# Layer norm at the end of a four-layer kernel: the variance by squares of the projection, gamma by GpSimd, and the residual added two pairs later

## The chip, the cores and the metric

One core of a Trainium2 chip runs one program over 16 images. The metric is the device time of one execution, in microseconds (us). The engines are PE (TensorE: matmuls, with weight loads as PEld), DVE (VectorE), ACT (ScalarE), POOL (GpSimd) and SP (SyncE, which here only issues DMAs). Each engine takes its instructions strictly in its own order; between engines there are semaphores.

## The reference

The input is `x`, 16 images of 64 x 64 pixels with 256 channels, float32. Four layers run one after the other, each as `x = x + layer(groupnorm(x))`. What the change touches is the last, linear attention with a layer norm:

```python
q, k, v = split(einsum('bxyc,cf->bxyf', x, w_qkv), 3)      # 128 channels each: 4 heads of 32
q = softmax(q, over the 32 channels of a head) * DIM_HEAD ** -0.5
k = softmax(k, over the 4096 pixels)
context = einsum('bhdn,bhen->bhde', k, v)
out = einsum('bhde,bhdn->bhen', context, q)
out = einsum('bxyh,hc->bxyc', out, w_out) + b_out
mu = mean(out, over the 256 channels); var = mean(square(out - mu))
out = (out - mu) * rsqrt(var + 1e-3) * gamma + beta
```

The layers before it: a search for the nearest of 1024 codes for each pixel, whose code is added (layer 0); an attention with sigmoids inside each row of 64 pixels (layer 1); and a gate from a softmax over 4096 x 4096 products of two rows, with which the pixel is multiplied (layer 2).

## The kernel before

Each image passes through generators, one for each stage: `stats0` (group norm statistics), `stage1` (search), `layer1`, `rows2`, `stage2` (the exponentials of layer 2), `gate2` and `stage3` (layer 3). A loop at the end of the kernel interleaves them. Every stage of every image has a start and a length written out by hand, every `yield` a weight, and the loop always continues the generator with the earliest due time. So five images are in work at once: while `stage3` finishes image 7, `gate2` works on image 8, `stage2` on image 9, `layer1` on image 10 and `stage1` on image 11. The scheduler of the language then settles the order in each engine's queue, near to the order of emission; work under `tc.high_priority` is pulled ahead. PE's order therefore has matmuls of four stages between two of `stage3`.

Tiles come from pools in which the tiles of one tag share a few buffers. In PSUM all stages share four banks of 128 x 512 float32 (`bank`) and two double banks (`wide`, for the search's distances and for layer 1).

A pixel set of 512 is a chunk; an image has eight. Images are kept in DRAM between the stages, channels on partitions (`x3` for `stage3`). `stage3` has two halves.

The first half goes over the chunks for keys, queries and values. With channels on partitions as weights, one matmul pair for each 128 pixels gives q and v side by side (L759). The group norm's mean comes in as a row that is added by a matmul with three rows of ones in bfloat16 (`ones3`, L763): `qv_row`, 256 wide, for two tiles at a time. ACT copies the bank to `qv` (L764, tag `u4`), POOL subtracts the maximum of each head (L779), ACT takes the exponential (L780), POOL multiplies by the reciprocal sum (L728), PE transposes q, and the result `qT` goes to DRAM (`qd`). The product of keys and values is summed up in `ctxa` (L784, L786).

Between the halves a short chain of URGENT steps (L797 to L817) transposes the context, masks it to the heads, multiplies it by `w_out`, scales it by the sum of the keys (`rk`, L805) and adds the bias `bo`. `w_out` and the bias were centred over the channels at the start, so the projection has mean zero, and its variance is the mean of its squares. Two forms of the weight are kept: `wctx[:, 0]` without gamma and `wctx[:, 1]` with it. From the first, two transposes and two matmuls make the Gram matrix `gram` = W W^T / 256.

The second half, the output half, goes over the chunks again. `form` (L822 to L828) loads the chunk's q, multiplies it by `gram` (`pz`, L826) and lets DVE multiply the product by q (`qz`, L828). `variance` (L830 to L837) sums this over the channels by a matmul with a column of ones (`pvr`, L834); ACT adds epsilon (L836) and POOL raises to -0.5 (L837): `rss`, the reciprocal deviation of each pixel. Both work one chunk ahead. Then, for each pair of 128-pixel tiles: PE projects with the weight that has gamma (`po`, L854), ACT scales each tile by its deviation on the way out of PSUM (L857, to `y`, tag `u4`), PE transposes the chunk of `x3` (`xo`) into a bank and adds the row `x_row` with beta (`pxo`, L859 and L863), and DVE adds both (L865). SP stores the chunk before (L867).

Outside layer 3 the change touches the search, `stage1`: for each tile of 128 pixels, ACT writes `nn` (L372), PE the distances `pd` (L377), DVE adds the two into `nd` and takes the maximum (L384), DVE finds its index (L389), and POOL issues the gather that adds the code row to the tile of pixels (L390). The pixels of a chunk are transposed back by PE (L352, `pt`) once its last gather has landed. `sq`, `nn`, `nd`, `fg` and `rows` share the tag `t4`; `qT`, `kx`, `ek` and `qz` share `v2`. In `stage2`, ACT and DVE take turns on 128 x 2048 exponentials: L617 on ACT, L620 on DVE with two inputs in SBUF.

Of the kernel before, what the change touches and what calls it, by code (L numbers as in the profile page):

```python
# [9 lines left out]
F32 = mybir.dt.float32  # L10
BF16 = mybir.dt.bfloat16
U32 = mybir.dt.uint32
AF = mybir.ActivationFunctionType
ALU = mybir.AluOpType
AX = mybir.AxisListType

P = 128
# [24 lines left out]
def kernel(  # L42
# [55 lines left out]
    neg_mat = s1p.tile([P, P], F32, tag="t4", name="neg_mat", bufs=5)  # L98
# [26 lines left out]
    def row_tile(name):  # L125
        t = const.tile([P, C], BF16, name=name)
        nc.gpsimd.memset(t, 0.0)
        return t

    h_row, qv_row, x_row = row_tile("h_row"), row_tile("qv_row"), row_tile("x_row")  # L130

    def twice(row):
        return row.unsqueeze(1).to_broadcast([P, 2, C])

    def put_row(dst, v, weight, tag, plus=None):
# [4 lines left out]
        row = pb[:PARTS, :C]  # L140
        weight(row, v3, plus)

        for n in range(PARTS - 1):
            top = small.tile([PARTS, C], BF16, tag="ptop", name=f"top_{tag}_{n}", bufs=1)
            nc.scalar.copy(top, row)
            nc.tensor.matmul(row, lhsT=below[:, n, :], rhs=top, start=False, stop=True, skip_group_check=True)
# [70 lines left out]
    for n in range(PARTS):  # L217
        nc.scalar.dma_start(out=bh3[:, :, n], in_=bh.rearrange("(k p) -> p k", p=P))
    one = const.tile([P, 1], F32, name="one")
# [83 lines left out]
    def stage1(b):  # L303
# [14 lines left out]
        def norm(ch):  # L318
            xn[ch] = s1p.tile([P, NK, CW], F32, tag="xn", name=f"xn_{tag}_{ch}")
            sq = s1p.tile([P, NK, CW], F32, tag="t4", name=f"sq_{tag}_{ch}", bufs=5)  # L320
# [46 lines left out]
        for ch in range(NCHUNK):  # L367
            for t in range(CH):
                T = ch * CH + t

                nn = s1p.tile([P, CODES], F32, tag="t4", name=f"nn_{tag}_{T}", bufs=5)
                nc.scalar.activation(nn, ne2, AF.Identity, bias=nx2[ch][:, t : t + 1])  # L372
                pd = wide(f"pd_{tag}_{T}")
                for hf in range(2):
# [7 lines left out]
                nd = s1p.tile([P, CODES], F32, tag="t4", name=f"nd_{tag}_{T}", bufs=5)  # L382
                m8 = m8s[T % 4]
                nc.vector.tensor_tensor_reduce(  # L384
                    out=nd, in0=pd, in1=nn, scale=1.0, scalar=-3.0e38, op0=ALU.add, op1=ALU.max,
# [3 lines left out]
                nc.vector.max_index(i8, m8, nd)  # L389
# [26 lines left out]
    def layer1(b):  # L416
# [34 lines left out]
        def attend(ch):  # L451
# [9 lines left out]
            fg = s1p.tile([2 * CK, 2, HW], F32, tag="t4", name=f"fg_{tag}_{ch}", bufs=5)  # L461
# [78 lines left out]
    def rows2(b):  # L540
# [17 lines left out]
        for h in range(2):  # L558
# [9 lines left out]
            rows = s1p.tile([P, CW], F32, tag="t4", name=f"rows_{tag}_{h}", bufs=5)  # L568
# [120 lines left out]
    def stage3(b):  # L689
# [9 lines left out]
        with tc.high_priority(offset=URGENT):  # L699
            scaled(wk_n, scale, nc.scalar)  # L700
            scaled(wqv_n, scale, nc.vector)
            put_row(qv_row, nmean, by_weight(wqv_n), f"qv_{tag}")
# [9 lines left out]
        def queries(ch):  # L712
# [4 lines left out]
            qT = s3p.tile([P, CW], F32, tag="v2", name=f"qT_{tag}_{ch}", bufs=4)  # L717
# [12 lines left out]
        for ch in range(NCHUNK):  # L730
# [14 lines left out]
            kx = s3p.tile([P, CW], F32, tag="v2", name=f"kx_{tag}_{ch}", bufs=4)  # L745
# [6 lines left out]
            qv = s3p.tile([P, CH, 2, P], F32, tag="u4", name=f"qv_{tag}_{ch}")  # L752
            qvs[ch] = qv
            for pr in range(CH // 2):
# [8 lines left out]
                nc.tensor.matmul(pqv, lhsT=ones3, rhs=twice(qv_row), start=False, stop=True, skip_group_check=True)  # L763
# [7 lines left out]
            ek = s3p.tile([P, CH, P], F32, tag="v2", name=f"ek_{tag}_{ch}", bufs=4)  # L771
# [23 lines left out]
        with tc.high_priority(offset=URGENT):  # L795
            pt = bank(f"pct_{tag}")
            nc.tensor.transpose(pt[:, :P], ctxa, ident)  # L797
            ctx_bd = wts.tile([P, P], F32, tag="ctx_bd", name=f"ctxbd_{tag}")
            nc.vector.tensor_tensor(ctx_bd, pt[:, :P], hmask, ALU.mult)
# [3 lines left out]

            wctx = wts.tile([P, 2, C], F32, tag="wctx", name=f"wctx_{tag}")
            nc.vector.scalar_tensor_tensor(wctx[:, 0, :], pw[:, :C], rk, bo, op0=ALU.mult, op1=ALU.add)  # L805
            nc.vector.tensor_tensor(wctx[:, 1, :], wctx[:, 0, :], gam, ALU.mult)

            pw = bank(f"pwt_{tag}")
            for k in range(NK):
                nc.tensor.transpose(pw[:, k * P : (k + 1) * P], wctx[:, 0, k * P : (k + 1) * P], ident)  # L810
            wT = wts.tile([P, NK, P], F32, tag="wk_n", name=f"wT_{tag}")
            nc.scalar.copy(wT.rearrange("p k d -> p (k d)"), pw[:, : NK * P])
            pw = bank(f"pgr_{tag}")
# [131 lines left out]
```

## Time and profile before

| what | us | where from |
|---|---|---|
| time, median of three runs | 5938.17 | runs from 5902.65 to 5948.46 |
| profiled execution | 5928.44 | its own time |
| its span | 5926.7 | first to last instruction |
| granted TensorE clock, mean | 0.941 | of full speed |
| first residual addition (L865) of images 7 and 8 | 3621.5 and 3972.8 | L865's row of starts |
| POOL's product with the query sums (L728), median and longest | 1.049 and 3.201 | L728's row |
| DVE's product with the exponentials (L620), median | 2.282 | L620's row |

How such a profile is read: for every engine it has the busy time and its share of the span, for every group of instructions (line, engine, operation, tiles) the count, the busy time, the mean duration and the idle time of the engine just before, with what ended it. A float32 matmul of this kernel shows as two passes, each with a weight load. A list of waits says which engine stood still for which other; a "window" is the same count for a stretch of the span. Busy shares are means over stages with different limits, so the stretches below are taken from one image's cycle.

In the middle of the span the cycle repeats for each image; the first image (before its followers start) and the last four (5005 us on) run with fewer partners.

### The profile page before, as it was taken

Reading aid. Unit: us, or ns where it says so; the run is one execution under the profiler, and the core shown is the slowest. Engines: PE = TensorE matmul, PEld = TensorE weight load, DVE = VectorE, ACT = ScalarE, POOL = GpSimd, SP = SyncE. Lnnn points to the kernel's source line nnn. Section 1 sums busy time; section 2 is a strip of 40 time slices with the busy share of each in tenths; the row PEclk is TensorE's granted clock in tenths of the full one; section 3 lists DMA queues with packets and bytes.
Section 4 is the critical chain, followed back from the end, with each engine's and each line's share of the span. In section 5 each row is a group of like instructions: output and inputs, shape, how many; then the busy total and the mean of one; then the engine's idle time right before and its main releaser. Section 6 shows DMA issues by size and latency. Waiting matters only on the chain.

```text
span 5926.7 us, 79561 instructions
## 1 busy us (share of the span) xinstructions
PE 5337.4 (90%) x28239; PEld 3211.1 (54%) x28239; DVE 5121.1 (86%) x7282; ACT 4570.8 (77%) x6754; POOL 1939.4 (33%) x1314
## 2 busy tenths in 40 slices
PE   8968899889999999998989999898999989997777
PEld 3524465545656565564656556565555646564555
DVE  6499798989989898898989889898998989888882
ACT  4377687878778787887879788797878878787873
POOL 3122233224233332433334233342424333231331
PEclk9989999989999898999999899999999999998899
DMA  6544745555656656565665656656565664644543
GB/s 186 162 124 124 225 137 177 184 184 162 207 168 192 197 151 202 184 207 181 184 205 167 194 183 188 206 174 204 164 210 164 202 204 147 209 158 173 184 158 116
DMA packets 521380, 1059.47 MB, mean 179 GB/s; under 512 B 52504, under 2 KB 266392, under 8 KB 512792
## 3 DMA queue, kind: packets, MB, share of 16 engines
q1 hardware_dynamic: 406288, 885.11, 44.7%
q0 software_dynamic: 73728, 67.14, 7.9%
q10 hardware_dynamic: 40968, 102.13, 4.5%
q8 instruction: 224, 3.67, 0.3%
q14 instruction: 172, 1.41, 0.1%
HBM read 751.18 MB, written 303.04 MB: 178 GB/s over the span
## 4 chain that ended last, share of the span: by engine, by line
PE 48%; DVE 16%; ACT 12%; DMA 7%; issue 6%; POOL 4%; ACTq 0%; SPq 0%; POOLq 0%; DVEq 0%
PE pd_s L377 15%; DVE ex_s L620 6%; ACT ex_s L617 5%; PE ph_l L468 5%; PE pqv_s L759 3%; PE po_s L854 3%; PE pk_s L737 3%; PE po_l L506 2%; PE pr_r L565 2%; DMA xr_r<-x_l 2%; DVE i_s L389 2%; POOL qv_s L779 2%; PE pvr_s L834 1%; PE pz_s L826 1%; DMA qo_s<-qd_s 1%
## 5 line engine op out<-in xcount | busy, mean ns | idle before, releaser
L620 DVE CUSTOM_DVE_ANT_0 ex_s<-ex_s,x2b 128x2048 f32<-128x2048 f32 x1024 | 2350.7, 2302 | 46.2 <-ACT ex_s L617 44.9
L617 ACT ACTIVATE ex_s<-x0b,nmax_s,x_r 128x2048 f32<-128x2048 f32 x1024 | 2137.8, 2088 | 66.4 <-DVE num_s L620 60.3
L377 PE MATMUL pd_s<-e,xn_s 128*128 128x512 f32 x4096 | 2022.2, 623 | 43.5 <-DVE m L384 40.8
L390 POOL DMA_INDIRECT xc_s<-in_emb_rows,i_s x512 | 1058.1, 2067 | 2063.9 <-DVE i_s L389 1466.8
L377 PEld LDWEIGHTS pd_s<-e,xn_s 128*128 128x128 f32 x4096 | 754.4, 197 | 764.9 <-issue 669.1
L384 DVE CUSTOM_DVE_ANT_0 nd_s<-pd_s,nn_s 128x1024 f32<-128x1024 f32 x512 | 622.2, 1215 | 174.4 <-ACT nn_s L372 82.1
L389 DVE FIND_INDEX8 i_s<-m,nd_s 128x8 uint32<-128x1024 f32 x512 | 624.1, 1219 | 0.0
L372 ACT ACTIVATE nn_s<-ne,nx_s 128x1024 f32<-128x1024 f32 x512 | 583.2, 1141 | 21.5 <-DVE nx_s L343 15.7
L468 PE MATMUL ph_l<-wh_l,xt_l 128*128 128x256 f32 x2048 | 525.5, 393 | 28.3 <-DVE m L384 16.5
L759 PE MATMUL pqv_s<-wqv_s,xk_s 128*128 128x256 f32 x2048 | 494.6, 382 | 0.0
L759 PEld LDWEIGHTS pqv_s<-wqv_s,xk_s 128*128 128x128 f32 x2048 | 390.9, 192 | 127.5 <-issue 65.5
L468 PEld LDWEIGHTS ph_l<-wh_l,xt_l 128*128 128x128 f32 x2048 | 380.9, 193 | 143.8 <-issue 57.5
L837 POOL TENSOR_TENSOR lrs_s<-lrs_s,mhalf 128x4 f32<-128x4 f32 x128 | 183.0, 1429 | 749.3 <-ACT lrs_s L836 710.5
L857 ACT ACTIVATE y_s<-po_s,lrs_s 128x256 f32<-128x256 f32 x512 | 237.1, 469 | 214.8 <-PE po_s L854 166.2
L854 PE MATMUL po_s<-wctx_s,qo_s 128*128 128x256 f32 x1024 | 336.0, 415 | 32.3 <-ACT y_s L857 31.1
L506 PE MATMUL po_l<-at_l,h_l 64*128 64x64 f32 x4096 | 318.5, 297 | 46.2 <-DVE xt_l L511 42.7
L506 PEld LDWEIGHTS po_l<-at_l,h_l 64*128 64x128 f32 x4096 | 286.5, 206 | 108.5 <-DVE xt_l L511 48.9
L779 POOL TENSOR_TENSOR qv_s<-qv_s,qm_s 128x512 f32<-128x512 f32 x128 | 232.7, 1818 | 312.3 <-DVE qm_s L778 181.7
L728 POOL TENSOR_TENSOR qv_s<-qv_s,qd_s 128x512 f32<-128x512 f32 x128 | 199.8, 1561 | 304.6 <-DVE qd_s L727 252.9
L865 DVE TENSOR_TENSOR y_s<-pxo_s,y_s 128x512 f32<-128x512 f32 x256 | 175.2, 686 | 125.0 <-ACT y_s L857 123.2
L854 PEld LDWEIGHTS po_s<-wctx_s,qo_s 128*128 128x128 f32 x1024 | 178.2, 198 | 172.5 <-ACT y_s L857 84.7
L737 PE MATMUL pk_s<-xk_s,wk_s 128*128 128x512 f32 x512 | 269.6, 650 | 0.0
(195 smaller groups left out, 7519.8 us busy)
## 6 DMA issues: line engine op xcount, KB each, us to landing
xs_s<-in_xT SPq DMA_DIRECT2D x128, 512.0 KB
xt_s<-in_xT SPq DMA_DIRECT2D x128, 512.0 KB
xc_s<-in_x SPq DMA_DIRECT2D x128, 512.0 KB
x_s<-xt_s ACTq DMA_DIRECT2D x128, 512.0 KB
xt_l<-x_s SPq DMA_DIRECT2D x128, 512.0 KB
x_l<-xt_l SPq DMA_DIRECT2D x128, 512.0 KB
xr_r<-x_l SPq DMA_DIRECT2D x128, 512.0 KB
xg_g<-x_l SPq DMA_DIRECT2D x128, 512.0 KB
```

The source lines that it names most:

```text
L372: nc.scalar.activation(nn, ne2, AF.Identity, bias=nx2[ch][:, t : t + 1])
L377: nc.tensor.matmul(pd[:, cols], lhsT=xn[ch][:, k, t * P : (t + 1) * P], rhs=e2[:, k, cols], start=(k == 0), stop=(k == NK - 1),)
L384: nc.vector.tensor_tensor_reduce(out=nd, in0=pd, in1=nn, scale=1.0, scalar=-3.0e38, op0=ALU.add, op1=ALU.max, accum_out=m8[:, 0:1],)
L389: nc.vector.max_index(i8, m8, nd)
L390: nc.gpsimd.indirect_dma_start(out=xc[ch][:, t, :], out_offset=None, in_=emb_rows, in_offset=bass.IndirectOffsetOnAxis(ap=i8[:, 0:1], axis=0),
L468: nc.tensor.matmul(ph[:, t, :], lhsT=X[:, k, t * P : (t + 1) * P], rhs=wh_n[:, k, :], start=(t % 2 == 0 and k == 0), stop=False, skip_grou ...
L506: nc.tensor.matmul(po[:, r, k * CH + t, :], lhsT=h[rows, t, k * P : (k + 1) * P], rhs=at[rows, t, :], start=True, stop=True,)
L617: nc.scalar.activation(ex, x0b, AF.Exp, bias=nmax[:, T : T + 1], scale=x01[:, T, 1:2], accum_out=den[:, h, T : T + 1])
L620: nc.vector.tensor_tensor_reduce(out=ex, in0=ex, in1=x2b, scale=1.0, scalar=0.0, op0=ALU.mult, op1=ALU.add, accum_out=num[:, h, T : T + 1],)
L737: nc.tensor.matmul(pk, lhsT=wk_n[:, k, :], rhs=xt[:, k, :], start=(k == 0), stop=(k == NK - 1))
L759: nc.tensor.matmul(pqv[:, j, :], lhsT=xt[:, k, t * P : (t + 1) * P], rhs=wqv_n[:, k, :], start=(j == 0 and k == 0), stop=False, skip_group ...
L854: nc.tensor.matmul(po[:, j, :], lhsT=qT[:, t * P : (t + 1) * P], rhs=wctx[:, 1, :], start=True, stop=True)
```

## The change

It does seven things.

1. The Gram matrix, `form` and `variance` are gone, with `wT`, `pz`, `qz` and `pvr`. The weight `wctx` is kept once, without gamma.
2. For each pair, `project` runs the projection, ACT copies the bank to `y`, and ACT takes the square of each tile with the sum over its row into `rs` (scale 1/16, so the mean of the squares), then adds epsilon.
3. POOL multiplies `y` by gamma (128 x 512) and raises the pair's two columns of `rs` to -0.5.
4. `add`, two pairs later (`LATE = 2`), loads and transposes `x3`, adds `x_row`, and DVE forms y * rs + px for each tile in one instruction.
5. v's mean is no longer added by a row to every tile: `vb`, a column, is added to the transposed context once per image, and `q_row` is 128 wide. `ctxa` is scaled by `rk` ahead of the transpose.
6. In the search, DVE's sum goes back into `nn`; `nd` is gone, and `t4` has four buffers instead of five.
7. `v2` has three buffers instead of four, `u4` three instead of two; `junk` takes the squares, which nothing reads.

```diff
-                nd = s1p.tile([P, CODES], F32, tag="t4", name=f"nd_{tag}_{T}", bufs=5)
                 m8 = m8s[T % 4]
                 nc.vector.tensor_tensor_reduce(
-                    out=nd, in0=pd, in1=nn, scale=1.0, scalar=-3.0e38, op0=ALU.add, op1=ALU.max,
+                    out=nn, in0=pd, in1=nn, scale=1.0, scalar=-3.0e38, op0=ALU.add, op1=ALU.max,
                     accum_out=m8[:, 0:1],
                 )
...
-                nc.vector.max_index(i8, m8, nd)
+                nc.vector.max_index(i8, m8, nn)
...
-            put_row(qv_row, nmean, by_weight(wqv_n), f"qv_{tag}")
+            put_row(q_row, nmean, by_weight(wqv_n[:, :, 0:P]), f"q_{tag}", cols=P)
+
+            pb = bank(f"pvb_{tag}")
+            for k in range(NK):
+                nc.tensor.matmul(
+                    pb[:, 0:1], lhsT=wqv_n[:, k, P:], rhs=nmean[:, k : k + 1], start=(k == 0), stop=(k == NK - 1)
+                )
+            vb = small.tile([P, 1], F32, tag="vb", name=f"vb_{tag}")
+            nc.scalar.copy(vb, pb[:, 0:1])
...
-                nc.tensor.matmul(pqv, lhsT=ones3, rhs=twice(qv_row), start=False, stop=True, skip_group_check=True)
+                nc.tensor.matmul(
+                    pqv[:, :, 0:P], lhsT=ones3, rhs=twice(q_row), start=False, stop=True, skip_group_check=True
+                )
...
+            nc.vector.tensor_scalar(ctxa, ctxa, rk, None, ALU.mult)
             pt = bank(f"pct_{tag}")
             nc.tensor.transpose(pt[:, :P], ctxa, ident)
             ctx_bd = wts.tile([P, P], F32, tag="ctx_bd", name=f"ctxbd_{tag}")
-            nc.vector.tensor_tensor(ctx_bd, pt[:, :P], hmask, ALU.mult)
+            nc.vector.scalar_tensor_tensor(ctx_bd, pt[:, :P], vb, hmask, op0=ALU.add, op1=ALU.mult)
...
-            pz = bank(f"pz_{tag}_{ch}")
-            nc.tensor.matmul(pz, lhsT=gram, rhs=qs[ch], start=True, stop=True)
-            prods[ch] = s3p.tile([P, CW], F32, tag="v2", name=f"qz_{tag}_{ch}", bufs=4)
-            nc.vector.tensor_tensor(prods[ch], pz, qs[ch], ALU.mult)
...
+        def project(ch, pr):
+
+            if pr == 0:
+                ys[ch] = s3p.tile([P, CH, C], F32, tag="u4", name=f"y_{tag}_{ch}", bufs=3)
+            y, qT = ys[ch], qs[ch]
+            po = bank(f"po_{tag}_{ch}_{pr}").rearrange("p (j c) -> p j c", c=C)
+            for j in range(2):
+                t = 2 * pr + j
+                nc.tensor.matmul(po[:, j, :], lhsT=qT[:, t * P : (t + 1) * P], rhs=wctx, start=True, stop=True)
+            two = y[:, 2 * pr : 2 * pr + 2, :]
+            nc.scalar.copy(two, po)
+            rs = rss[ch, pr] = small.tile([P, 2], F32, tag="ln_rs", name=f"lrs_{tag}_{ch}_{pr}", bufs=4)
+            for j in range(2):
+                nc.scalar.activation(
+                    junk, po[:, j, :], AF.Square, scale=float(C ** -0.5), accum_out=rs[:, j : j + 1]
+                )
+            nc.gpsimd.tensor_tensor(two, two, gam.unsqueeze(1).to_broadcast([P, 2, C]), ALU.mult)
+            nc.scalar.activation(rs, rs, AF.Identity, bias=eps3)
+            nc.gpsimd.tensor_tensor(rs, rs, mhalf[:, 0:2], ALU.pow)
+
+        def add(ch, pr):
+
+            if pr == 0:
+                xts[ch] = xb.tile([P, NK, CW], F32, tag="xb", name=f"xo_{tag}_{ch}")
+                nc.sync.dma_start(out=xts[ch], in_=x3[ch])
...
+            nc.tensor.matmul(px, lhsT=ones3, rhs=twice(x_row), start=False, stop=True, skip_group_check=True)
+            rs = rss.pop((ch, pr))
+            for j in range(2):
+                v = ys[ch][:, 2 * pr + j, :]
+                nc.vector.scalar_tensor_tensor(v, v, rs[:, j : j + 1], px[:, j, :], op0=ALU.mult, op1=ALU.add)
+
+        fetch(0)
+        yield 4
+        LATE = 2
+        for i in range(2 * NCHUNK + LATE):
+            ch, pr = divmod(i, 2)
+            if ch < NCHUNK:
+                project(ch, pr)
+                if pr == 0 and ch + 1 < NCHUNK:
+                    fetch(ch + 1)
+            if i >= LATE:
+                ch, pr = divmod(i - LATE, 2)
+                if pr == 0 and ch > 0:
+                    nc.sync.dma_start(out=dst[:, (ch - 1) * CH : ch * CH, :], in_=ys.pop(ch - 1))
+                add(ch, pr)
+            yield 3
```

In the changed kernel the lines that the prediction names are L832 (projection), L834 (copy), L837 (squares), L840 (gamma), L842 (power), L861 (scaled addition), L353 (transposes of the search) and, as before, L617 and L620.

## The prediction

> **What bounds the kernel now.** I read the busy totals first, then the chain, then one image in two stretches, then the waits inside the first stretch, last the rows that price the edit.
>
> ```profile
> PE 5337.4 (90%) x28239; PEld 3211.1 (54%) x28239; DVE 5121.1 (86%) x7282; ACT 4570.8 (77%) x6754; POOL 1939.4 (33%) x1314
> ...
> PE 48%; DVE 16%; ACT 12%; DMA 7%; issue 6%; POOL 4%; ACTq 0%; SPq 0%; POOLq 0%; DVEq 0%
> ```
>
> Two engines are nearly full and half of the chain is PE, but no line of it stands out (L377 has most, 15%). The residual additions (L865) of image 7 run from 3621.5 to 3739.3 us and those of image 8 start at 3972.8, so an image takes 351 us, of which the output half of layer 3 holds 117. The windows view splits it there:
>
> ```profile
> core 0: us, PE busy (x) PEld busy (x) DVE busy (x) ACT busy (x) POOL busy (x), PEclk, DMA share, GB/s
> ...
> 3622.00:3739.00 117.00, 107.73 (x639) 71.84 (x639) 103.05 (x142) 86.66 (x134) 29.60 (x18) 0.94 0.72 222
> 3739.00:3973.00 234.00, 219.90 (x1129) 126.86 (x1127) 213.19 (x311) 197.57 (x289) 93.86 (x63) 0.97 0.55 172
> ```
>
> In both stretches PE is 92 to 94% busy and DVE 88 to 91%. ACT differs: 74% in the output window, 84% outside. The edit puts its work into ACT's emptier stretch. DVE idles 14 us of those 117; its waits there, and ACT's:
>
> ```profile
> DVE y_s L865 <- ACT y_s L857: 6.2, 4, 3.4
> DVE qz_s L828 <- PE pz_s L826: 3.7, 2, 3.1
> DVE nd_s L384 <- ACT nn_s L372: 3.0, 2, 1.8
> ...
> ACT y_s L857 <- PE po_s L854: 14.2, 9, 4.1
> ACT lrs_s L836 <- PE pvr_s L834: 5.4, 4, 2.7
> ```
>
> So 9.9 of DVE's 14 idle microseconds are waits of the two DVE steps that the edit removes.
>
> **The prices** (line, engine, tiles, count, busy us, mean ns, idle before):
>
> ```profile
> L857 ACT ACTIVATE y_s<-po_s,lrs_s 128x256 f32<-128x256 f32 x512 | 237.1, 469 | 214.8 <-PE po_s L854 166.2 <-POOL lrs_s L837 40.1 <-issue 3.9
> L779 POOL TENSOR_TENSOR qv_s<-qv_s,qm_s 128x512 f32<-128x512 f32 x128 | 232.7, 1818 | 312.3 <-DVE qm_s L778 181.7 <-DVE nkm_s L740 35.9 <-PE pt_s L352 35.8
> L837 POOL TENSOR_TENSOR lrs_s<-lrs_s,mhalf 128x4 f32<-128x4 f32 x128 | 183.0, 1429 | 749.3 <-ACT lrs_s L836 710.5 <-ACT xrow_s L336 13.2 <-ACT grow_s L640 12.0
> L865 DVE TENSOR_TENSOR y_s<-pxo_s,y_s 128x512 f32<-128x512 f32 x256 | 175.2, 686 | 125.0 <-ACT y_s L857 123.2 <-PE pxo_s L863 1.4
> L764 ACT COPY qv_s<-pqv_s 128x512 f32<-128x512 f32 x256 | 146.1, 578 | 61.6 <-PE pqv_s L763 60.2
> L828 DVE TENSOR_TENSOR qz_s<-pz_s,qo_s 128x512 f32<-128x512 f32 x128 | 87.3, 682 | 53.0 <-PE pz_s L826 52.7
> L746 ACT ACTIVATION_READ_ACCUMULATOR kx_s<-pk_s,nkm_s 128x1 f32 x128 | 24.8, 194 | 0.0
> L805 DVE SCALAR_TENSOR_TENSOR wctx_s<-pw_s,rk_s,bo 128x256 f32<-128x256 f32 x16 | 7.7, 482 | 3.5 <-PE pw_s L802 3.1
> L812 ACT COPY wT_s<-pwt_s 128x256 f32<-128x256 f32 x16 | 5.9, 369 | 9.2 <-PE pwt_s L810 9.2
> ```
>
> **What the Trainium skill says.** "Perfetto Trace Analysis", Identifying the Most-Contended Engine: matmul busy time is no measure of PE's headroom, because matmuls overlap. The trace agrees: L377's passes last 623 ns each but 2022.2 us/4096 = 494 ns of busy time, and its weight loads follow 0.43 us apart. I price PE by spacing, not by mean. "SBUF — State Buffer", Who interferes with whom: a DVE instruction with two SBUF inputs and a GpSimd instruction that reads SBUF lock each other out. The trace agrees: L728 on POOL has a median of 1049 ns and a longest of 3201, the longer ones beside L620 (2282 ns, both inputs in SBUF). "GPSIMD Engine Reference", Key points: GpSimd can't access PSUM, which is why ACT's copy has to stand ahead of POOL's gamma; no run here shows this.
>
> **Part by part, per image of 16.**
>
> PE loses work. Eight gram products are two passes each at 0.43 us (6.9 us). 32 variance columns are 64 weight-load-bound passes; eight take 0.95 us at 3007.0 us in the timeline, so 7.6. The 16 added rows of 512 bf16 columns (0.22 us by spacing) shrink to 256, saving 0.11 each, 1.8, outside the output window. The two transposes and the gram in the context chain go, about 1; four tiny passes for v's mean come, under 0.5. In the output window PE falls from 107.7 to about 93.
>
> ACT: out go 32 scalings x 0.469 = 15.0 and 8 epsilon steps x 0.260 = 2.1. In come 16 copies 128x512 x 0.578 = 9.2; 32 squares; 16 epsilon steps x 0.260 = 4.2. A square with accumulation isn't in the trace: L812's plain 256-column copy out of PSUM (0.369) is the floor, L857 (0.469) the ceiling, plus 0.194 to read the accumulator. I take 0.42 + 0.19 = 0.61, since the scale is a constant, not a tile; 19.5 (18.0 to 21.2). Net +15.8 (14.3 to 17.5): 86.7 becomes 102.5. The 0.6 us of wT (L812) and gram (L817) saved per image lie between the windows.
>
> DVE: out go 16 additions x 0.686 = 11.0 and 8 products x 0.682 = 5.5. In come 32 scaled additions 128x256, one input in PSUM: 0.40 (the 398 ns of L806, two tensors without a scalar) to 0.482 (L805); I take 0.46, 14.7. POOL's gamma adds locks: with its 256 products of today, the instances of L620 and L675 that start behind one exceed their usual length by about 30 us in all, so 256 more cost about 2 per image (0 to 4). Net 0: DVE stays at 103. Two small steps more and less in the context chain cancel.
>
> POOL: 16 gamma products at 1.05 (free) to 3.1 (behind L620), taken at 1.8 as L779: 29. Powers of 128x2 go from 8 x 1.43 to 16 x about 1.0 (L270's mean): +5. POOL rises from 29.6 to about 63 of 117: not full. What queues behind it are gathers (L390), in order; twice as many POOL steps now wait for ACT there. Of the gathers that end a chunk, those of tiles 15 and 19 fall into the output window; they landed about 17 and 4 us ahead of their transposes (L352) in eight of nine middle images. A few microseconds are thus covered; uncovered, they are PE's. I take 0 (0 to +2).
>
> Waits: L865's and L828's 9.9 us go, as deviation and row sum are now two pairs (some 14 us) old when DVE adds. New is that a bank of the projection is held for a copy and two squares (1.8 us) instead of two scalings (0.94); but a chunk now takes four banks instead of six. I leave it at 0 (-1 to +3). The rewritten search output (nn in place, four buffers instead of five) removes a buffer per tile; the v2 tag loses its fourth buffer with its fourth user; u4 gains one. Nothing in the waits names these buffers: 0 (-1 to +1). SP issues as many loads and stores as before; the load of x3 (xo) and the store of a chunk move two pairs later, with the transposes and additions that they serve, a few places down SP's order past loads of the search and of layer 1, and the store has the third u4 buffer: 0. ACT's queue keeps its DMAs.
>
> **How the numbers follow.** After, ACT 102.5 and DVE 103 share the output window with PE at 93. Three engines cannot fill it: PE's best now is 94%. At 93% for DVE it lasts 111 instead of 117: of the 9.9 us of waits about 4 come back as waits for a fuller ACT. Outside, PE's 1.8 us count nearly whole. 8 us x 16 = 128. The profiled execution has a span of 5926.7 us in 5928.4: that gives 5800. The median of the three runs lies 9.8 above it, so **5810**.
>
> **Rivals.**
> 1. *PE alone set the pace.* For: 48% of the chain. Against: DVE would have to be 95% busy. Then all 17 us count: 272, 5665. Chance 0.13.
> 2. *The waits are replaced.* ACT's fuller queue hands DVE all 9.9 us back, as waits for nn, ex and the copies; the window stays at 117 and only 2 us outside remain: 32, 5905. For: ACT and DVE take turns on ex (L617 and L620). Chance 0.21.
> 3. *ACT becomes the bound, slower.* Squares stand between ex and nn in ACT's order, so whatever PE and DVE wait for behind them comes later. With squares at their ceiling (0.66) ACT has 104.2 us; its best share in either stretch today is 84%, and if that is its limit the window lasts 104.2/0.84 = 124. That is 7 more, x 16 = 112, less the 32 outside: +80, 6020. The gain is gone once ACT cannot hold 104.2/119 = 88%. Against: most of ACT's idle time there is waiting for PE (14.2 and 5.4 us), and PE gets lighter. Chance 0.16.
> 4. *The edit doesn't do what it says.* The built order shows the gram products gone and projections two pairs ahead of their additions; no chance given.
>
> My forecast holds 0.50. About 1% is what a measurement of this kernel can tell from no change. Faster by over 1%: forecast and rival 1, 0.63; within: 0.21; slower: 0.16. The range reaches down to rival 1 and up part of the way to rival 3: 5670 to 5975.
>
> **What would show it.** PE's busy time down by about 250 us, ACT's up by about 240, POOL's by 500, DVE's within 40; no wait of L861 on ACT worth over 2 us per image; output windows near 111 us, the rest near 232. Wrong: DVE's waits for nn or ex (L617) up by over 5 us per image, long waits for the squares' banks, transposes L353 waiting for gathers, or squares above 0.48 us.

## The result: slower, and where the time went

The changed kernel takes 6008.66 us (median of four runs, 5987.52 to 6027.14) against 5940.53 for the kernel before on the same chip: ratio 1.0134 (95% interval 1.0087 to 1.0182). The forecast was 5810, with a range that ended at 5975. The profiled execution has a span of 6002.1 us and a mean granted clock of 0.912 (0.941 before).

The busy totals of the changed kernel, and the windows of its image 7 (first to last L861, then to image 8's first; columns as in the prediction):

```profile
PE 5167.7 (86%) x26927; PEld 3106.9 (52%) x26927; DVE 5173.4 (86%) x7410; ACT 4680.2 (78%) x7634; POOL 2438.1 (41%) x1698
```

```profile
3678.00:3787.00 109.00, 95.74 (x536) 62.29 (x537) 105.02 (x153) 85.97 (x165) 53.68 (x38) 0.88 0.71 221
3787.00:4040.00 253.00, 223.86 (x1148) 129.90 (x1146) 215.99 (x308) 204.93 (x313) 101.00 (x68) 0.94 0.55 167
```

By this count the output window did what was forecast: 109 us, with DVE 96% busy in it, and the stretch outside, expected at 232, has 253. But the two stretches no longer hold the same work. With the addition two pairs late, two more pairs of projections stand before the first addition, and so in the stretch outside. The projections of image 7, first of the kernel before, then of the changed one (the last figures are the first and last start):

```profile
L854 PE MATMUL po_s<-wctx_s,qo_s x64: 379/379/793, 3614.5 to 3731.0; 128*128 128x256 f32 x64
```

```profile
L832 PE MATMUL po_s<-wctx_s,qo_s x64: 379/379/634, 3652.1 to 3759.0; 128*128 128x256 f32 x64
```

The first addition comes 7 us after the first projection in the kernel before and 26 us after it in the changed one. From the last addition of image 7 to the first projection of image 8 both kernels take 226.5 us. For this image, then, the loss lies where the output half is at work, together with the four other stages: 135.4 us from the first projection to the last addition, where the kernel before has 124.9. The waits of DVE over the whole changed kernel:

```profile
DVE x_r L575 <- PE prt_r L574: 141.9, 29, 11.4
DVE ex_s L620 <- ACT ex_s L617: 113.8, 76, 6.3
DVE nn_s L384 <- PE pd_s L378: 77.0, 40, 10.1
DVE nn_s L384 <- ACT nn_s L373: 66.6, 39, 5.9
DVE wqv_s L283 <- POOL s_n L271: 60.0, 16, 7.4
DVE y_s L861 <- POOL lrs_s L842: 46.9, 36, 7.9
DVE st_s L250 <- ACT xt_s L356: 45.2, 17, 5.0
```

The same list of the kernel before, in part:

```profile
DVE x_r L575 <- PE prt_r L574: 110.8, 31, 11.6
...
DVE ex_s L620 <- ACT ex_s L617: 44.9, 50, 2.3
...
DVE wqv_s L282 <- POOL s_n L270: 19.8, 16, 3.1
DVE st_s L249 <- ACT xt_s L355: 18.8, 23, 3.8
```

The 123.2 us of L865's wait for ACT and the 52.7 of L828's are gone. In their place L620 waits 69 us more for ACT, the scaled weights (wqv) 40 more for a POOL power, the group norm statistics (st) 26 more for the tile that ACT copies out of the transposes, and the new addition 47 for its deviation from POOL. But waits alone don't explain it; DVE also works longer. Rows of DVE and POOL, first of the kernel before, then of the changed one:

```profile
L620 DVE CUSTOM_DVE_ANT_0 ex_s<-ex_s,x2b 128x2048 f32<-128x2048 f32 x1024 | 2350.7, 2302 | 46.2 <-ACT ex_s L617 44.9
```

```profile
L620 DVE CUSTOM_DVE_ANT_0 ex_s<-ex_s,x2b 128x2048 f32<-128x2048 f32 x1024 | 2434.7, 2383 | 115.3 <-ACT ex_s L617 113.8 <-issue 1.2
...
L840 POOL TENSOR_TENSOR y_s<-y_s,gam 128x512 f32<-128x512 f32 x256 | 413.7, 1625 | 394.0 <-ACT y_s L834 367.3 <-DMA gb_g<-gd_s 14.5 <-ACT junk L837 7.2
...
L842 POOL TENSOR_TENSOR lrs_s<-lrs_s,mhalf 128x2 f32<-128x2 f32 x256 | 339.2, 1399 | 137.3 <-ACT lrs_s L841 67.2 <-issue 54.7 <-ACT ex_s L617 7.2
...
L861 DVE SCALAR_TENSOR_TENSOR y_s<-y_s,lrs_s,pxo_s 128x256 f32<-128x256 f32 x512 | 221.7, 467 | 72.5 <-POOL lrs_s L842 46.9 <-PE pxo_s L857 20.5 <-POOL y_s L840 3.4
```

The same 1024 L620 instructions take 84 us more (2434.7 - 2350.7). Two figures thus have to be explained, DVE's idle time and its own lengthening. A table counts both for each run, from each trace's own instructions: an image's output window from the first to the last start of its residual addition, and the rest up to the next image's first; means of images 4 to 11, counted from 0; DVE busy in both together.

| kernel | window | rest | DVE busy | DVE idle: window | rest |
|---|---|---|---|---|---|
| before | 115.2 | 233.8 | 313.8 | 12.3 | 22.9 |
| changed | 110.4 | 245.2 | 317.1 | 5.5 | 33.0 |
| before, search edit alone | 114.4 | 246.5 | 317.9 | 11.9 | 31.1 |
| before, sum in place, nn in two buffers | 114.5 | 242.7 | 318.7 | 12.0 | 26.5 |
| before, late fused add alone | 107.9 | 242.0 | 317.4 | 9.6 | 22.9 |
| changed, separate sum | 111.9 | 243.8 | 321.6 | 5.8 | 28.3 |
| changed, no gamma | 104.3 | 240.7 | 310.6 | 2.7 | 31.7 |
| changed, POOL scalar | 105.8 | 240.9 | 311.5 | 3.7 | 31.5 |
| two projections | 108.4 | 240.7 | 311.8 | 6.6 | 30.7 |
| two projections, separate sum | 108.3 | 241.5 | 316.1 | 6.4 | 27.3 |

(all in us per image)

The last three columns add up over the whole cycle. Window and rest can be compared only between kernels whose addition stands at the same distance from the projection, for the reason given above. Counted from the first matmul of the output half (the Gram product, or the projection where there is none) to its last addition, the same images give (a cycle counted from another start differs by up to 1 us):

| kernel | output half | rest |
|---|---|---|
| before | 129.1 | 219.5 |
| changed | 135.1 | 221.5 |
| before, late fused add alone | 137.1 | 212.2 |
| changed, no gamma | 125.8 | 219.7 |
| two projections | 129.7 | 219.6 |

So the changed kernel's output half is 6 us longer than before, not shorter, and the rest 2 us longer.

### The profile page after: what moved, and what is told of

It reads as the page before. It is cut to its first block, busy times and chain, and to the rows that moved or that the text cites. A ratio compares the mean times of both kernels' runs of the same rounds, so it can differ in the third digit from the quotient of the medians.

```text
span 6002.1 us, 78576 instructions
## 1 busy us (share of the span) xinstructions
PE 5167.7 (86%) x26927; PEld 3106.9 (52%) x26927; DVE 5173.4 (86%) x7410; ACT 4680.2 (78%) x7634; POOL 2438.1 (41%) x1698
## 5 line engine op out<-in xcount | busy, mean ns | idle before, releaser
L620 DVE CUSTOM_DVE_ANT_0 ex_s<-ex_s,x2b 128x2048 f32<-128x2048 f32 x1024 | 2434.7, 2383 | 115.3 <-ACT ex_s L617 113.8
L617 ACT ACTIVATE ex_s<-x0b,nmax_s,x_r 128x2048 f32<-128x2048 f32 x1024 | 2140.5, 2091 | 73.9 <-DVE num_s L620 61.3
L378 PE MATMUL pd_s<-e,xn_s 128*128 128x512 f32 x4096 | 2044.0, 634 | 66.8 <-DVE m L384 43.6
L378 PEld LDWEIGHTS pd_s<-e,xn_s 128*128 128x128 f32 x4096 | 769.2, 201 | 864.8 <-issue 726.1
L384 DVE CUSTOM_DVE_ANT_0 nn_s<-pd_s,nn_s 128x1024 f32<-128x1024 f32 x512 | 619.1, 1213 | 153.8 <-PE pd_s L378 77.0
L389 DVE FIND_INDEX8 i_s<-m,nn_s 128x8 uint32<-128x1024 f32 x512 | 622.2, 1216 | 0.1
L840 POOL TENSOR_TENSOR y_s<-y_s,gam 128x512 f32<-128x512 f32 x256 | 413.7, 1625 | 394.0 <-ACT y_s L834 367.3
L842 POOL TENSOR_TENSOR lrs_s<-lrs_s,mhalf 128x2 f32<-128x2 f32 x256 | 339.2, 1399 | 137.3 <-ACT lrs_s L841 67.2
L832 PE MATMUL po_s<-wctx_s,qo_s 128*128 128x256 f32 x1024 | 303.5, 425 | 45.6 <-ACT at_l L493 17.0
L789 POOL TENSOR_TENSOR qv_s<-qv_s,qm_s 128x512 f32<-128x512 f32 x128 | 170.5, 1332 | 364.1 <-DVE qm_s L788 247.8
L861 DVE SCALAR_TENSOR_TENSOR y_s<-y_s,lrs_s,pxo_s 128x256 f32<-128x256 f32 x512 | 221.7, 467 | 72.5 <-POOL lrs_s L842 46.9
L832 PEld LDWEIGHTS po_s<-wctx_s,qo_s 128*128 128x128 f32 x1024 | 204.7, 212 | 123.2 <-issue 60.9
```

The source lines that it names most:

```text
L378: nc.tensor.matmul(pd[:, cols], lhsT=xn[ch][:, k, t * P : (t + 1) * P], rhs=e2[:, k, cols], start=(k == 0), stop=(k == NK - 1),)
L384: nc.vector.tensor_tensor_reduce(out=nn, in0=pd, in1=nn, scale=1.0, scalar=-3.0e38, op0=ALU.add, op1=ALU.max, accum_out=m8[:, 0:1],)
L389: nc.vector.max_index(i8, m8, nn)
L617: nc.scalar.activation(ex, x0b, AF.Exp, bias=nmax[:, T : T + 1], scale=x01[:, T, 1:2], accum_out=den[:, h, T : T + 1])
L620: nc.vector.tensor_tensor_reduce(out=ex, in0=ex, in1=x2b, scale=1.0, scalar=0.0, op0=ALU.mult, op1=ALU.add, accum_out=num[:, h, T : T + 1],)
L832: nc.tensor.matmul(po[:, j, :], lhsT=qT[:, t * P : (t + 1) * P], rhs=wctx, start=True, stop=True)
```

## The experiments

The ratio of each run is to the kernel before on the same chip, with its 95% interval. The runs were made on several chips; the medians of the kernel before lie between 5925.6 and 5940.5 us on them. A cost is given as the difference of two medians. The interval of the changed kernel's own ratio is 28 us to each side, so a cost counted against it is known to some 30 us. Line numbers move by one or two where an edit adds or removes lines, and of each edit only the lines that matter are shown.

### What in the changed kernel costs

Three explanations stand against each other in what was expected; the first expectation says what the lock, ACT and clock theories are.

**POOL's product taken away.**

```diff
-            nc.gpsimd.tensor_tensor(two, two, gam.unsqueeze(1).to_broadcast([P, 2, C]), ALU.mult)
```

> The changed kernel without POOL's product with gamma (L840); the output lacks gamma. Lock theory (POOL's product and DVE's L620, both reading SBUF, shut each other out): L620's mean falls from 2383 ns back to near 2302, its busy time by 60 to 80 us, and the time falls from about 6008 to 5900-5940. ACT theory (copies and squares make ACT late, and DVE and PE with it): nothing on ACT is removed, so the time stays within 25 us of 6008. Clock theory (PE, with less work, idles often enough to lose its clock, and that eats the gain): POOL's product is no part of it, so cold time stays near 1050 us and the time near 6008.

Gamma is left out. 5859.82 us, 0.9881 (0.9845 to 0.9917): the product costs 149 us, where the ACT and clock theories expected no change and the lock theory less, and without it the kernel is faster than the kernel before. L620 is near its old length, and DVE is busy 6.5 us less per image:

```profile
L620 DVE CUSTOM_DVE_ANT_0 ex_s<-ex_s,x2b 128x2048 f32<-128x2048 f32 x1024 | 2363.5, 2313 | 103.0 <-ACT ex_s L617 102.6
```

**The squares taken away**, the deviation from a constant (the variance is left out).

```diff
-                nc.scalar.activation(
-                    junk, po[:, j, :], AF.Square, scale=float(C ** -0.5), accum_out=rs[:, j : j + 1]
-                )
...
-            nc.scalar.activation(rs, rs, AF.Identity, bias=eps3)
+            nc.scalar.activation(rs, mhalf[:, 0:2], AF.Identity, scale=-2.0, bias=eps3)
```

> The changed kernel without ACT's squares (L837); the deviation is a constant in the output. It takes about 306 us of work (199 + 107) off ACT. ACT theory: the time falls by over 100 us, to 5850-5900, and DVE's waits for L617 (114 us) fall to the 45 us of before. Lock theory: L620 stays at 2370-2390 ns and the time stays above 5970. Clock theory: cold time stays above 950 us and the time above 5950.

5959.46 us, 1.0052 (1.0038 to 1.0066): the squares cost some 49 us, a third of the product. That is less than the ACT theory expected and a little more than the lock theory did; the clock theory's ranges hold it. L620 stays at 2365 ns, and its wait for ACT falls only to 81.7 us.

**More work for PE**: one more matmul of 512 columns per pair.

```diff
+            warm = bank(f"warm_{tag}_{ch}_{pr}")
+            nc.tensor.matmul(warm, lhsT=ident, rhs=qT, start=True, stop=True)
```

> The changed kernel with one matmul of 128x512 that nothing reads added to each pair: 256 x 2 passes x 0.43 us = 220 us of PE work, nearly what the change took from PE. If PE's work set the time: 6008 + 150 to 220 = 6160-6230. Clock theory: PE idles less, cold time falls from 1053 us towards 700, and the time stays within 40 us of 6008 or falls. Lock theory: L620 stays near 2383 ns and the time near 6008, or a little above.

5994.76 us, 1.0093 (1.0063 to 1.0124), no slower than the changed kernel. The clock paid for a part: the time in which the records have the granted clock at 0.5 fell from 1053 to 843 us, which saves PE some 105 us (an estimate: half of the 210). The other half of the 220 us cost nothing. So PE's work does not set the changed kernel's time; what PE's relief, the prediction's largest removal, brings by itself in the kernel before was not run.

### Why the product costs

The first two tries replaced the product by POOL work that depends on nothing: three memsets, or gamma times gamma into a spare tile, each per pair.

> The changed kernel with the product with gamma replaced by three POOL memsets of 128x512 on a tile that nothing reads (at least as long as the 1.26 us of a free product, but reading nothing from SBUF); the output lacks gamma. Lock theory: a POOL instruction that only writes doesn't shut L620 out, so L620 stays below 2330 ns and the time comes out like the run without the product, 5850-5900. POOL-queue theory (gathers and norm factors stand behind POOL's longer queue): the time stays at 5970-6020, with L620 near 2313.

> The changed kernel with POOL's product made of gamma with itself into a tile that nothing reads, so that it waits for no copy and no addition waits for it; the output lacks gamma. Lock theory: it still reads SBUF, so L620 stays at 2360-2390 ns and the time at 5960-6020. Chain theory (the product between ACT's copy and DVE's addition makes the addition late): 5850-5890, as without the product.

5964.33 us, 1.0069 (1.0045 to 1.0093), and 6031.64, 1.0174 (1.0133 to 1.0214). Neither tells the theories apart: without operands to wait for, POOL did all of the work in the first 627 and 352 us (an expectation below has 590 for the first), ahead of its real work, and the search of image 3 (from 0) found its first index 124 and 182 us later than in the kernel before. By the last image that had fallen to 83 and 144. So both were repeated with operands that hold the work in the output half: four memsets of the tile that took the squares, or q times q from the chunk's q, whose result nobody reads. All four leave gamma out.

```diff
...
+            for _ in range(4):
+                nc.gpsimd.memset(jk, 0.0)
```

> The changed kernel with the product with gamma replaced by four POOL memsets of 128x256 over the tile that the squares have just been written to, so that they stand in the output half of each image (the earlier memsets, which waited for nothing, had all been run in the first 590 us); the output lacks gamma. Lock theory: they read nothing, L620 stays below 2330 ns, time 5850-5890. POOL-queue theory (about 300 us of POOL time in the same place delays gathers and factors): 5950-6020 with L620 near 2315.

```diff
+            nc.gpsimd.tensor_tensor(spare.rearrange("p j c -> p (j c)"), qT, qT, ALU.mult)
```

> The changed kernel with the product with gamma replaced by a POOL product of the chunk's q with itself into a tile that nothing reads, so that it stands in the output half and reads SBUF, but no addition waits for it; the output lacks gamma. Lock theory: L620 at 2360-2390 ns, DVE busy near 5170 us, time 5960-6020. Chain theory (DVE's addition waits for the product): 5850-5890.

Memsets: 5902.38 us, 0.9957 (0.9936 to 0.9978), 43 above the run without a product; L620 stays at 2313 ns. Product of q: 5929.28, 1.0002 (0.999 to 1.0013), 69 above it; L620 rises to 2343, DVE's busy time to 5129 us. Both times fall between the ranges of the two theories. POOL's time in its queue costs something; for about the same time on POOL (360 and 396 us busy) the product costs more, and it alone shows in DVE, though less than the lock theory expected.

The cleanest test keeps the step, its place and every queue's order, and changes only the operation: POOL multiplies y by 1 in place of gamma, which is left out.

```diff
-            nc.gpsimd.tensor_tensor(two, two, gam.unsqueeze(1).to_broadcast([P, 2, C]), ALU.mult)
+            nc.gpsimd.tensor_scalar(two, two, 1.0, None, ALU.mult)
```

> The changed kernel with POOL multiplying y by the constant 1 in place of gamma: the same step in the same chain, copy to POOL to the late add, but one SBUF operand in place of two. If the two operands cost because DVE's L620 runs beside them: the instances of L620 longer than 2.34 us fall from 129 to under 50, L620 from 2383 to about 2320 ns, and the time to 5890 to 5940 us. If the step costs by its place in the chain and in POOL's queue: 5970 to 6020 us.

5912.21 us, 0.9965 (0.9948 to 0.9981), 96 below the changed kernel. Its rows:

```profile
L620 DVE CUSTOM_DVE_ANT_0 ex_s<-ex_s,x2b 128x2048 f32<-128x2048 f32 x1024 | 2369.8, 2319 | 93.9 <-ACT ex_s L617 93.4
...
L840 POOL TENSOR_SCALAR y_s<-y_s 128x512 f32<-128x512 f32 x256 | 530.8, 2104 | 324.4 <-ACT y_s L834 312.3 <-ACT xt_s L356 7.7 <-DVE xg_g L675 3.1
```

POOL's own step is longer (2104 ns against 1625), and the kernel is faster: the length of POOL's step is not what costs here, and DVE is busy 76.5 us less (5173.4 - 5096.9). In the changed kernel 85 of the L620 instructions beside L840 take longer than 2.34 us, 71.3 us in all above 2.285; here 29, 7.5 us. The expected count of all long L620 (under 50) was missed, at 73: the other 44 lie beside POOL steps that the edit didn't touch. Of the product's 149 us, 96 go with the product's form and 52 (5912.21 - 5859.82) with having a step there at all, in the chain and in POOL's queue.

The Trainium skill ("SBUF — State Buffer", Who interferes with whom) has a DVE instruction with two SBUF inputs contend with any GpSimd instruction that reads SBUF, and the order of issue decide who is blocked. The product agrees: of those 85 long L620 instructions 82 started after the product beside them, and the product takes 1.83 us in the mean beside L620 and 1.36 away from it. The multiplication by 1 reads SBUF too, but there POOL paid nearly all (2.41 us beside L620, 1.65 away from it). Whether the number of operands or the kind of operation makes the difference, no run here separates.

### The same product in the kernel before, and the search edit by itself

The kernel before has no room in SBUF for the spare tile that such a product writes, so the product could not be tried in it alone. The search edit (the sum back into nn, four buffers) frees that room, and the edit by itself was run to compare with.

> The kernel before with the search edit alone (sum into nn, tag t4 with four buffers). Predicted at nothing: the time within 15 us of 5930. If the fewer buffers hold ACT's nn or sq up, DVE's wait of L384 for ACT rises above 82 us and the time by 20 us or more.

> The kernel before with the search edit and one POOL product of the chunk's q with itself for each pair, into a tile that nothing reads, standing in the output half. Lock theory: against the search edit alone L620's mean rises by 60 to 80 ns, DVE's busy time by 60 to 90 us and the time by 80 to 150 us. ACT theory and clock theory: the time stays within 20 us of the search edit alone.

The edit by itself was the surprise: 6068.42 us, 1.026 (1.0219 to 1.0301), 143 us for an edit costed at nothing. With q times q per pair on POOL it takes 6126.91, 1.0338 (1.031 to 1.0366), another 58, close to the 69 in the changed kernel. L620 rises from 2323 to 2345 ns and DVE's busy time by 39 us: more than the ACT and clock theories allow, and less than the lock theory expected in all three figures. Waits of DVE with the search edit alone:

```profile
DVE nn_s L383 <- PE pd_s L377: 93.8, 64, 11.6
DVE nn_s L383 <- ACT nn_s L372: 91.2, 63, 3.7
DVE ex_s L619 <- ACT ex_s L616: 72.3, 49, 3.2
DVE st_s L249 <- ACT xt_s L355: 53.9, 37, 3.8
...
DVE qd_s L725 <- ACT qv_s L779: 35.9, 28, 5.8
```

Against the kernel before the sums wait 31 us more for the distances, L620's line 27 more for ACT, the statistics 35 more, the query sums 16 more. The loss is spread thinly; no wait names the buffer. The table has it as 8.2 us more idle per image in the rest, and 4.1 us more of busy DVE.

**Its two halves.** First four buffers with the separate sum, then the sum in place with five.

```diff
-                nd = s1p.tile([P, CODES], F32, tag="t4", name=f"nd_{tag}_{T}", bufs=5)
+                nd = s1p.tile([P, CODES], F32, tag="t4", name=f"nd_{tag}_{T}", bufs=4)
```

> The kernel before with the t4 tag cut from five buffers to four and nothing else; the search keeps its separate sum nd. Splits the search edit (6068 against 5926 us with both halves). If the count costs, because squares, gates and rows wait for a buffer: 6040 to 6120 us, the more so as a tile still takes two. If it is the sum in place that costs: 5915 to 5960 us.

```diff
-                    out=nd, in0=pd, in1=nn, scale=1.0, scalar=-3.0e38, op0=ALU.add, op1=ALU.max,
+                    out=nn, in0=pd, in1=nn, scale=1.0, scalar=-3.0e38, op0=ALU.add, op1=ALU.max,
...
```

> The kernel before with the search's sum written over nn, five buffers kept. If the count costs: 5910 to 5945 us. If the sum in place costs, because ACT may now write nn two tiles further ahead and so stands in front of other ACT work: 6050 to 6100 us, with more nn ahead than in the run with four buffers.

5930.99 us, 0.9993 (0.9979 to 1.0007), and 6092.34, 1.0282 (1.0242 to 1.0322). The fifth buffer is worth nothing; with four the order of every queue is the same as with five. The sum in place costs all of it, and it moves instructions on every engine. It lets nn run ahead: in the kernel before, 16 of 512 sums found a further nn already written, here 92, of which 26 found two or more.

**Is it the lead?** nn in two buffers of its own, in place, can lead by one tile at most.

```diff
-                nn = s1p.tile([P, CODES], F32, tag="t4", name=f"nn_{tag}_{T}", bufs=5)
+                nn = s1p.tile([P, CODES], F32, tag="nn", name=f"nn_{tag}_{T}", bufs=2)
...
```

> The kernel before with the sum in place, nn in two buffers of its own and three left for the other t4 tiles, so that ACT can write at most one nn ahead of the sum, as it does with a separate sum. If the in-place sum costs because it lets nn run two and more tiles ahead and so ahead of other ACT work (in the run with five buffers 92 of 512 sums have one or more nn ahead, in the kernel before 16): 5915 to 5970 us. If it costs because the buffer is held until max_index, or because any other order of the queues is worse than the one the kernel before was given: 6040 to 6110 us.

6041.13 us, 1.0181 (1.0141 to 1.0221): 115 of the cost stay. The idle time in the rest falls (26.5 us per image, where the sum in place with five shared buffers has 33.8), and L620 is longer (2356 ns). No sum found two further nn written, so most of the cost comes without leads of two tiles and more. But 96 still found one: the lead wasn't brought back to the 16 of the kernel before, and this run doesn't decide between a lead of one, the buffer held until the index is found, and the new order as such. That stays open.

**Undone inside the changed kernel.** nd restored, four buffers.

> The changed kernel with the separate sum nd restored, still with four buffers. If the sum in place costs here what it costs in the kernel before (about 140 us): 5850 to 5900 us. If four buffers are the cost, or if the cost belongs to the old output half only: 5990 to 6080 us.

5989.15 us, 1.0099 (1.0065 to 1.0133), where 5850 to 5900 would have meant that the cost carries over whole; it stops 1 us short of the other range. The intervals of this ratio and of the changed kernel's overlap; the gain is about 19 us if any, though the sums that found a further nn fell from 91 to 13. The table shows where it goes: idle in the rest falls by 4.7 us per image, but DVE is busy 4.5 more. Its costliest row:

```profile
L621 DVE CUSTOM_DVE_ANT_0 ex_s<-ex_s,x2b 128x2048 f32<-128x2048 f32 x1024 | 2481.8, 2429 | 77.1 <-ACT ex_s L618 76.8
```

The exponentials' step takes 2429 ns instead of 2383, 47 us in all, and waits 37 us less for ACT. What the separate sum gives in waits, the exponentials lose again in length; why they get longer no run here shows.

### The waiting part alone, and what beats both

**Late fused add in the kernel before**: gram variance, weight with gamma and search as they were; ACT copies the pair, and DVE scales and adds two pairs later.

```diff
-                    nc.scalar.activation(y[:, t, :], po[:, j, :], AF.Copy, scale=rs[:, t : t + 1])
+            nc.scalar.copy(y[:, 2 * pr : 2 * pr + 2, :], po)
...
+                nc.vector.scalar_tensor_tensor(v, v, rss[ch][:, t : t + 1], px[:, j, :], op0=ALU.mult, op1=ALU.add)
```

> The kernel before with its gram variance, its weight with gamma and its search, but ACT copies the projected pair without waiting for the variance and DVE scales and adds it two pairs later. This is the waiting part of the change without its squares, its POOL product and its search edit. Prediction's steps alone: 9.9 us of waits an image go, about 2 come back, DVE gains 3 us of adds: 5810 to 5870 us. If the waits are taken over by others, as in the changed kernel: 5900 to 5960 us.

5903.02 us, 0.9961 (0.995 to 0.9971): 23 us, not 55 to 115. The window shrinks by 7.3 us and the rest grows by 8.2; DVE's idle time in the window falls only from 12.3 to 9.6. A shorter window is no gain by itself: two pairs of projections now lie ahead of the first addition, and work that left the window is done in the rest. The middle images gain nothing; the 23 us come from the end, where the time from the first addition of image 12 on falls from 567.1 to 535.9 us.

**Two projections**: PE projects each pair twice, with the plain weight for the squares and with the weight times gamma for y. No product on POOL; all else as in the changed kernel.

```diff
+            for j in range(2):
+                t = 2 * pr + j
+                nc.tensor.matmul(pg[:, j, :], lhsT=qT[:, t * P : (t + 1) * P], rhs=wgam, start=True, stop=True)
...
-            nc.scalar.copy(two, po)
+            nc.scalar.copy(two, pg)
...
-            nc.gpsimd.tensor_tensor(two, two, gam.unsqueeze(1).to_broadcast([P, 2, C]), ALU.mult)
```

> Complete in its output: PE projects twice, without gamma for the squares and with gamma for the copy; POOL multiplies nothing. 220 us of PE work more than the changed kernel, POOL's product gone. Lock theory, with PE not the bound (the added matmul cost nothing): L620 near 2313 ns, DVE busy near 5085 us, 5840-5890 us, faster than before. If PE sets the time once the locks are gone: 5950 or more.

5888.49 us, 0.9926 (0.9905 to 0.9947). It beats both kernels, and lies in the range of the lock theory; L620 is at 2316 ns. Two variants: ACT scales the second projection by the deviation, one pair later, and DVE only adds; and the separate sum with the squares written back into their PSUM bank.

> As the two projections, but ACT scales the second one by the deviation on its way out (512 x 469 ns for 256 x 585 ns, 90 us more) one pair late, and DVE adds the pair in one 128x512 step (256 x 686 ns for 512 x 467 ns, 63 us less busy). If DVE's busy time sets the time: DVE near 5025 us, and 5780-5850 us. ACT theory: 90 us more on ACT and a wait of DVE for ACT in the same step make it slower than the two projections, above 5880.

> The run with two projections (5888 us) with the separate sum nd restored at four buffers, and the squares written back into their own PSUM bank in place of the spare tile. If the sum in place costs: 5740 to 5830 us, the fastest of all. If it doesn't: 5880 to 5960 us.

5948.54 us, 1.004 (1.0027 to 1.0053): DVE was lighter (5058.6 us busy against 5091.5), but its L620 waited 165.1 us for ACT instead of 109.0. And 5882.41, 0.9917 (0.9884 to 0.9949), the same as the first within the intervals: as in the changed kernel, the waits that the separate sum saves (3.6 us per image) return as longer DVE work (4.3).

## Why the prediction was wrong

**What held.** The window between the first and the last addition: forecast 117 to 111, measured 115.2 to 110.4 over the middle images. DVE's idle time there fell by 6.8 us, forecast 5.9. That the window's length fits is in part luck: without the product it is 104.3. Prices of the new steps held: copy 0.585 us (0.578), fused add 0.467 (0.46), product 1.625 (1.8); POOL's power of 128x2 was too low (1.0, measured 1.399). POOL's busy time rose by 499 us (500 forecast).

ACT was forecast too full: 102.5 us of the window, measured 87.9. A square lasts 0.389 + 0.209 = 0.598 us (0.61), but in the trace it overlaps its neighbours on ACT, so that the durations of ACT's instructions rise by 256 us in sum and its busy time by 109 only. PE's busy time fell by 170 instead of 250; DVE's rose by 52, beyond the 40. The forecast's own signs of being wrong hardly showed: DVE's wait for ex (L617) rose by 4.3 us per image, its wait for nn fell, and PE's wait of the transposes (L353) for gathers rose from 57.1 to 72.2 us in all.

**What failed is the step from the window to the image**: "8 us x 16 = 128", with "the rest near 232". The rest measured 245.2, 13 us per image or 211 in 16, about the size of the miss (199). Three terms made it up.

1. The 6 us of the shorter window were counted as 6 us of a shorter cycle, and the two pairs of projections that now stand before the first addition were charged to nobody. The waiting part alone shows it: the window gives 7.3 us, the rest takes 8.2, and the kernel gains 23 us where 55 to 115 were expected. In the changed kernel without the product the rest still has 240.7. Nor did "PE's 1.8 us count nearly whole" show: in the changed kernel added PE work cost nothing.
2. "256 more cost about 2 per image (0 to 4)", within a DVE sum of "net 0": mis-sized. The L620 instructions beside L840 alone are 71.3 us longer, 4.5 per image, and DVE is busy 6.5 per image more than without the product. I took the excess beside today's POOL products (L728, L779) as typical of 256 more; it wasn't. With the chain and the queue, costed at nothing, the product comes to 149 us, 9.3 per image. By the table 6.1 of its cost per image lie in the window and 4.5 in the rest.
3. "Nothing in the waits names these buffers: 0": wrong for the sum in place, right for the buffer count. A wait list shows what a buffer costs today; it didn't show what a freed buffer does to the order of the queues. The kernel before loses 143 us by this edit. In the changed kernel it can't be added to term 2: undone there, it gives about 19 if any, since what the waits lose L620 takes back in length.

The terms are not a sum: each was measured in another kernel, and the squares, some 49 us, overlap with them. Without the product the changed kernel is 69 us faster than the kernel before, so the product is what turned a gain into a loss.

**The rivals.** That PE alone sets the pace does not hold in the changed kernel, by the run with more PE work. That the waits are replaced was the nearest, with the waits for ex, st and wqv in their place, but too small, since it had no term for DVE's lengthening. That ACT becomes the bound had the right side and nearly the right time (6020) for a wrong reason: ACT is busy 87.9 of the window's 110.4 us, 80%, and without the squares the window is no shorter (111.5).

## What to carry to other kernels

When a step moves to GpSimd, price it first by the other engine: which DVE instructions with two SBUF inputs run at that time, and what they lose, since a longer GpSimd step that left DVE nearly alone was 96 us faster here. A shorter stretch is a gain only if the cycle gets shorter: when a step is delayed, a window that begins with it begins later too, so bound the window by the same work before and after, and add up DVE's busy and idle time over the whole cycle. And an output written over its input can change the order of all queues, as it did here: run such an edit alone before it is bundled.

## What was not expected of the hardware

With less work PE ran longer at a lower clock: with the gram products gone, the time in which the records have the granted clock at 0.5 rose from 702 to 1053 us. Weight loads of the distances (L378) mostly follow at 429 ns at the full clock and at 850 in those stretches. The run with more PE work has 843 us, the two projections 718. But the amount of PE's work is not all: without POOL's product, with PE's work as in the changed kernel, it is 844. The Trainium skill ("TensorE: Matmul & The Clock Gate", Part 1: The HAM clock gate) makes the clock depend on how busy PE has been just before, which fits; no run here shows how much of the total the lower clock costs.
